# Where the work beside attention stands in the PE queue: between scores and values instead of after them

## The chip, the cores and the metric

The kernel runs on one core of a Trainium2 chip. The metric is device time in microseconds (us); the kernel before was timed three times, and 11980.78 us is the median (11979.94 to 11983.56). DMA moves data between HBM and the on-chip memories SBUF and PSUM. Engines are named as the profile does: PE (TensorE, matmuls), PEld (its weight loads), ACT (ScalarE), DVE (VectorE), POOL (GpSimd) and SP (SyncE, which here only issues DMAs). All data are float32.

## The reference, cut to what matters

Four images of 4096 tokens with 128 channels go through three layers: a state-space scan in three directions, an attention block with a small feed-forward part, and a mixture of 64 experts that pools tokens and scatters answers back. The change touches the attention block and what runs beside it:

```python
heads = u.reshape(4, 4096, 16, 8)                  # u: normalised tokens
q = qz_ring(heads + rx_theta)                      # cosines and running products
scores = einsum('bhsd,bhtd->bhst', q, q) / sqrt(8) # 16 heads, 4096 x 4096 each
attn = softmax(scores)
ctx = einsum('bhst,bhtd->bhsd', attn, q)
x1 = norm(u + ctx @ w_comb.T + b_comb)
zf = cos(x1[..., :8]) * cos(ry_theta)
x2 = norm(x1 + relu(zf @ w1.T + b1) @ w2.T + b2)   # then the layer's residual, norm, and gate logits
```

## The kernel before, in words

The program is written by one Python routine, `tile_kernel`, and the order in which instructions are recorded is the order in each engine's queue. It first makes the inputs of all scans and runs the scan of image 0, then the opening (angles, rings, queries) of image 0. Then come four attention loops, one for each image (`Attention.loop`). In the first three, the scan and opening of the next image and the closing work of the previous one are recorded beside the attention rounds. In the last (image 3) what runs beside it is the closing work of image 2 (`block.after(2)`), the choice and pooling of experts for images 0 to 2 (`Experts.search`, `choice`, `gather`), and the closing work of image 3 itself for those blocks of 512 queries that are done. After the loops come the last block's closing work and the experts' answers; I call it the tail.

One loop has 1024 rounds. A round treats four heads, 512 queries and 128 keys. `scores(i)` issues four matmuls (L955) into two PSUM tiles of two banks each, and for each tile one ACT exponential of 128x1024 (L960). `values(i)` issues four float32 matmuls (eight instructions in the trace, L969) which accumulate 32 rounds of one (head group, query block) pair in the one-bank tile acc. After the 32nd, `sums` copies acc to SBUF (L978, on ACT) and three rounds later stores it (L984, L987). The PSUM has three score tiles (six banks), one acc bank, and one bank for everything beside the rounds (`Bank`). The order within round i is: scores(i+1), values(i), sums, then `beside(i)`. So scores are one round ahead of values, and the exponential of round i+1 follows that of round i in ACT's queue.

Work beside is written as generators. Each `yield` is a step; a generator that is about to issue PE work yields the mark `PE`. `Bank.take` gives such a mark and waits until the bank is free. `flow` interleaves two such generators. `Pace.run(share)` adds a share to a credit and takes whole steps while there is credit: in the last loop 0.92 of a step in each round, whatever kind the step is.

A piece of PE work is all that one step issues. Pieces in the last loop, by name: co (L1072, two matmuls, 30 pieces), zt (L1093, four transposes, 15), h (L1107, one matmul of 8x512, 60), fo (L1118, four matmuls, 60), xT (L1140, four transposes, 14), lg (L1150, one matmul, 14), wt and pool (L1285 and L1296, four matmuls each, 24 of each). The scan's pieces in the first three loops are y (L582). Producers and consumers of these pieces are mostly on DVE: the norm (L836 to L842, with two POOL instructions at L48 and L49), products, and evictions from PSUM.

Of the kernel before, what the change touches and what calls it, by code (L numbers as in the profile page):

```python
# [16 lines left out]
P = 128  # L17
C = 128
L = 4096
NT = L // P  # L20
# [12 lines left out]
QB = 512  # L33
# [51 lines left out]
PE = "pe"  # L85
# [596 lines left out]
class Attention:  # L682
# [3 lines left out]
    def __init__(self, tc, ctx, w, gate, cols, ident, bank, dram, t1, w_out, sums, sz, x):  # L686
        nc = self.nc = tc.nc
        gate_w, gate_b = gate
        self.tc, self.cols, self.ident, self.bank, self.dram, self.t1 = tc, cols, ident, bank, dram, t1
        self.w_out, self.sums, self.sz, self.x = w_out, sums, sz, x  # L690
        const = ctx.enter_context(tc.tile_pool(name="a_const", bufs=1))
        self.half_pi = column(nc, const, math.pi / 2.0, "a_half_pi")

        def rows(name, n):
            t = const.tile([P, n], F32, name=f"bc_{name}")
            nc.scalar.dma_start(out=t, in_=w[name].partition_broadcast(P))
            return t

        self.theta = rows("rx_theta", D)
        self.bc = {k: rows(k, C) for k in ("b_comb", "b2", "g1", "beta1", "g2", "beta2")}  # L700
        self.b1 = const.tile([P, 4], F32, name="b1")
        nc.scalar.dma_start(out=self.b1, in_=w["b1"].rearrange("(f p) -> p f", p=P))
        self.cos_ry = const.tile([D, 3], F32, name="cos_ry")
        nc.scalar.dma_start(out=self.cos_ry[:, 0:1], in_=w["ry_theta"].unsqueeze(1))
        cosine(nc, self.cos_ry[:, 2:3], self.cos_ry[:, 0:1], self.cos_ry[:, 1:2], self.half_pi)
        self.w_comb = const.tile([P, C], F32, name="w_comb")
        self.w1 = const.tile([D, FFN], F32, name="w1")
        self.w2 = const.tile([P, 4, C], F32, name="w2")

        self.gate = const.tile([P, E], F32, name="gate")  # L710
        self.gate_b = const.tile([2 * E, 1], F32, name="gate_b")
        for k in range(2):
            nc.scalar.dma_start(out=self.gate_b[k * E : (k + 1) * E], in_=gate_b.unsqueeze(1))
        with tc.tile_pool(name="a_load", bufs=1) as load, tc.tile_pool(
            name="a_load_ps", bufs=2, space=PSUM
        ) as load_ps:
            raw = load.tile([P, C], F32, name="raw_comb")
            nc.sync.dma_start(out=raw, in_=w["w_comb"])
            ps = load_ps.tile([P, 512], F32, tag="ps", name="ps_comb")
            nc.tensor.transpose(ps[:, :C], raw, ident)  # L720
            nc.vector.tensor_copy(self.w_comb, ps[:, :C])
            raw = load.tile([P, 4, D], F32, name="raw_w1")
            nc.sync.dma_start(out=raw, in_=w["w1"].rearrange("(f p) d -> p f d", p=P))
            ps = load_ps.tile([P, 512], F32, tag="ps", name="ps_w1")
            for f in range(4):
                nc.tensor.transpose(ps[:D, f * P : (f + 1) * P], raw[:, f, :], ident)
            nc.vector.tensor_copy(self.w1, ps[:D])
            raw = load.tile([P, FFN], F32, name="raw_w2")
            nc.sync.dma_start(out=raw, in_=w["w2"])
            ps = load_ps.tile([P, 512], F32, tag="ps", name="ps_w2")  # L730
            for f in range(4):
                nc.tensor.transpose(ps[:, f * P : (f + 1) * P], raw[:, f * P : (f + 1) * P], ident)
            nc.vector.tensor_copy(self.w2.rearrange("p f c -> p (f c)"), ps)
            raw = load.tile([E, C], F32, name="raw_gate")
            nc.scalar.dma_start(out=raw, in_=gate_w)
            ps = load_ps.tile([P, 512], F32, tag="ps", name="ps_gate")
            nc.tensor.transpose(ps[:, :E], raw, ident[:E, :E])
            nc.vector.tensor_copy(self.gate, ps[:, :E])
        self.small = ctx.enter_context(tc.tile_pool(name="a_small", bufs=2))
        self.u, self.q, self.v, self.context, self.total, self.t2 = {}, {}, {}, {}, {}, {}  # L740
        self.xn, self.logits, self.angled, self.whole, self.closed = {}, {}, {}, {}, {}
        self.lag = 0
        self.round = column(nc, const, ROUND, "round"), column(nc, const, -ROUND, "minus_round")

    def begin(self, loop):
# [27 lines left out]
    def tokens(self, b, g, angles):  # L773


        nc = self.nc
# [6 lines left out]
        for m in range(2):  # L783
            rows = slice(m * P, (m + 1) * P)
# [35 lines left out]
        turned(nc, a, turns.rearrange("p h d -> p (h d)"), self.round if self.n == 4 else None)  # L820
        self.angled[b] += 1
        yield

    def settle(self, n=1):

# [80 lines left out]
    def loop(self, b, beside, by_block=False):  # L906


        nc = self.nc
        self.context[b] = self.dram.tile([P, L], F32, name=f"d_ctx_{b}")  # L910
        self.total[b] = self.dram.tile([L // QB, H, QB], F32, name=f"d_sum_{b}")
        self.whole[b] = 0
# [62 lines left out]
        def sums(j, qb, i):  # L975

            av = self.mid.tile([P, QB], F32, tag="av", name=f"av_{b}_{j}_{qb}")
            nc.scalar.copy(av, accs.pop((j, qb)))  # L978
            cut = slice(qb * QB, (qb + 1) * QB)

            def store():
                for k in range(4):
                    h = 4 * k + j
                    nc.gpsimd.dma_start(  # L984
                        out=self.context[b][h * D : h * D + D, cut], in_=av[32 * k : 32 * k + D, :]
                    )
                nc.gpsimd.dma_start(  # L987
                    out=self.total[b][qb].rearrange("(k j) t -> j k t", j=4)[j], in_=av[D::32, :]
                )
                if by_block and j == 3:  # L990
                    self.whole[b] = qb + 1

            later[i + 3] = store
# [5 lines left out]
        for i, (j, qb, kc) in enumerate(rounds):  # L999
            if i % 4 == 0:  # L1000
                fetch(i // 4 + 3)
            if i + 1 < len(rounds):
                scores(i + 1)
            values(i)
            if kc == NT - 1:
                sums(j, qb, i)
            if kc == NT - 12 and i + 12 < len(rounds):
                masked(*rounds[i + 12][:2])
            if i in later:
                later.pop(i)()  # L1010
            beside(i)
        for i in sorted(later):
            later[i]()
        self.whole[b] = L // QB

    def after(self, b, gs=range(L // QB), to=None):
# [68 lines left out]
        def second(g):  # L1085
# [4 lines left out]
            nc.sync.dma_start(out=t, in_=tiles[:, cut, :])  # L1090
            ps = yield from self.bank.take(f"zt_{b}_{g}")
            for k in range(4):
                nc.tensor.transpose(ps[:D, k * P : (k + 1) * P], z[:, g * 4 + k, :], self.ident)  # L1093
            yield
            zT = self.piece([D, 512], "p0", name=f"zT_{b}_{g}")
# [8 lines left out]
            h = self.one.tile([P, 4, 512], F32, tag="h", bufs=max(1, self.n - 1), name=f"h_{b}_{g}")  # L1104
            for f in range(4):
                ps = yield from self.bank.take(f"h_{b}_{g}_{f}")
                nc.tensor.matmul(ps, self.w1[:, f * P : (f + 1) * P], zT, start=True, stop=True)  # L1107
                yield
                if self.n == 2:
                    nc.vector.tensor_scalar(h[:, f, :], ps, self.b1[:, f : f + 1], 0.0, ALU.add, ALU.max)  # L1110
                else:
                    nc.scalar.activation(h[:, f, :], ps, AF.Relu, bias=self.b1[:, f : f + 1])
                self.bank.leave()
            yield from self.settle()
            for k in range(4):
                ps = yield from self.bank.take(f"fo_{b}_{g}_{k}")
                for f in range(4):
                    nc.tensor.matmul(  # L1118
                        ps[:, :C], h[:, f, k * P : (k + 1) * P], self.w2[:, f, :], start=(f == 0), stop=(f == 3)
                    )  # L1120
                yield
                nc.vector.tensor_add(u[:, k, :], u[:, k, :], ps[:, :C])
                self.bank.leave()
# [13 lines left out]
            yield from self.settle()  # L1137
            ps = yield from self.bank.take(f"xT_{b}_{g}")
            for k in range(4):
                nc.tensor.transpose(ps[:, k * P : (k + 1) * P], u[:, k, :], self.ident)  # L1140
            yield
            xT = self.piece([P, 512], "p0", name=f"xT_{b}_{g}")
# [4 lines left out]
            yield from self.settle()  # L1147
            ps = yield from self.bank.take(f"lg_{b}_{g}")
            rows = slice(E, 2 * E) if to else slice(0, E)
            nc.tensor.matmul(ps[rows], self.gate, xT, start=True, stop=True)  # L1150
            yield
            if to:
                for t in to:
# [283 lines left out]
class Pace:  # L1437


    def __init__(self, *parts):  # L1440
        self.parts, self.credit, self.done, self.then = chain(*parts), 0.0, False, None

    def run(self, share):
        self.credit += share
        while self.credit >= 1 and not self.done:
            self.credit -= 1
            self.then = next(self.parts, self)
            self.done = self.then is self

    def rest(self):  # L1450
        while not self.done:
# [3 lines left out]
def tile_kernel(tc, ctx, x, in_proj_w, dirs, out_proj_w, attn, gate, weight1, weight2, out):  # L1455


    nc = tc.nc
# [81 lines left out]
    with tc.manual_schedule():  # L1540
# [6 lines left out]
            block.after(nb - 1, range(0, 4)), block.after(nb - 1, range(4, 6)), block.after(nb - 1, range(6, blocks - 1)),  # L1547
            experts.search(pairs[-1], blocks - 1),
        )
        block.loop(nb - 1, lambda i: last.run(0.92), True)  # L1550
        last.rest()
    loop.close()
    with ExitStack() as end:
        block.bank = Bank(end.enter_context(tc.tile_pool(name="end_ps", bufs=7, space=PSUM)), 7)
# [47 lines left out]
```

## Time and profile before

The profile is of one execution, whose own time was 11985.97 us; its span from first to last instruction is 11984.3 us. Times inside the profile count from the span's start.

| stretch (us from start) | length | PE busy | DVE busy | ACT busy | granted PE clock |
|---|---|---|---|---|---|
| first loop, 2437 to 4831 | 2394 | 2223 | 2058 | 2326 | 0.98 |
| second loop, 4876 to 7248 | 2372 | 2245 | 2065 | 2299 | 0.98 |
| third loop, 7292 to 9620 | 2328 | 2219 | 1889 | 2260 | 0.98 |
| last loop, 9622 to 11734 | 2112 | 2071 | 361 | 1940 | 1.00 |
| tail, 11734 to 11984 | 250 | 128 | 86 | 32 | 0.67 |

"Busy" is the time in which at least one instruction of the engine is recorded as running. Matmuls overlap and their ends are modelled, so a busy PE may still have room. In the timeline, a line gives the start, how long the merged run of instructions lasted, the engine, the code line, operation, output<-input, and in brackets how long the engine was idle before it and what ended that. In lists of waits, a line says which engine's which line waited for which, the total, the count and the longest.

### The profile page before, as it was taken

The numbers are of one execution on the slowest core, as the hardware profiler recorded it, in microseconds if no ns is written. First come the engines' busy times: TensorE is split into PE (matmuls) and PEld (weight loads), VectorE is DVE, ScalarE is ACT, GpSimd is POOL, SyncE is SP. The second block draws the span as 40 slices with busy tenths as digits, with TensorE's granted clock in tenths as the row PEclk, the third lists the DMA queues.
The fourth block names the chain that finished last, engine by engine and source line by source line (L and its number), as shares of the span: only waits on it lengthen the run. The fifth ranks groups of instructions, "written<-read, shape, count | busy, mean of one in ns | idle before, by whom it ended". The sixth has DMA issues, their size and how long they took to land.

```text
span 11984.3 us, 184513 instructions
## 1 busy us (share of the span) xinstructions
PE 10801.0 (90%) x69190; PEld 3648.6 (30%) x69190; DVE 8666.3 (72%) x8841; ACT 10457.4 (87%) x10884; POOL 3068.7 (26%) x4017
## 2 busy tenths in 40 slices
PE   7898888489999999899999998999999999999995
PEld 3333333222222222233333222233332223333323
DVE  6999999889888877898889878989898321101123
ACT  5776777389999999899999988999999999999992
POOL 2323243222232322323334223233232110100011
PEclk9898989699999999999999999999999999999997
DMA  5666666655656565665565655655555332222125
GB/s 159 206 185 181 188 177 187 199 159 151 157 150 158 136 163 162 166 158 151 145 152 141 158 169 165 156 147 148 144 144 134 123 109 67 74 69 78 61 71 182
DMA packets 835831, 1747.64 MB, mean 146 GB/s; under 512 B 141070, under 2 KB 373574, under 8 KB 834678
## 3 DMA queue, kind: packets, MB, share of 16 engines
q1 hardware_dynamic: 649438, 1318.65, 41.5%
q0 software_dynamic: 144000, 307.48, 8.2%
q10 hardware_dynamic: 41496, 109.71, 3.5%
q8 instruction: 543, 8.90, 0.3%
q14 instruction: 354, 2.90, 0.1%
HBM read 1379.76 MB, written 355.47 MB: 145 GB/s over the span
## 4 chain that ended last, share of the span: by engine, by line
PE 62%; ACT 12%; issue 9%; DVE 8%; DMA 7%; SPq 1%; POOL 0%; ACTq 0%; DVEq 0%; POOLq 0%
PE acc L969 31%; PE s L955 15%; ACT e L960 7%; PE y L582 5%; DVE h L550 3%; PE cv L390 3%; PE sp L448 3%; DMA delta<-d_delta 2%; PE fo L1118 1%; PE xd L404 1%; PE h L1107 1%; DMA y<-d_y 1%; DVE dB L541 1%; ACT dA L534 1%; ACT delta L534 1%
## 5 line engine op out<-in xcount | busy, mean ns | idle before, releaser
L960 ACT ACTIVATE e<-s 128x1024 f32<-128x1024 f32 x8192 | 7778.6, 1102 | 366.5 <-PE s L955 322.0
L969 PE MATMUL acc<-e,val 128*32 128x512 f32 x32768 | 5681.9, 614 | 79.7 <-ACT av L978 79.0
L955 PE MATMUL s<-qm,key 32*128 32x512 f32 x16384 | 2783.4, 501 | 373.2 <-ACT e L960 311.5
L955 PEld LDWEIGHTS s<-qm,key 32*128 32x128 f32 x16384 | 1067.2, 183 | 3628.7 <-issue 1953.2
L552 POOL COPY ends<-h 128x1 f32<-128x1 f32 x1152 | 1299.0, 1130 | 2685.2 <-DVE h L550 2682.1
L969 PEld LDWEIGHTS acc<-e,val 128*32 128x32 f32 x32768 | 1027.7, 109 | 2007.6 <-issue 1015.7
L550 DVE TENSOR_TENSOR_SCAN h<-delta,ends,du 128x1024 f32<-128x1024 f32 x576 | 1349.6, 2343 | 113.8 <-ACT delta L534 95.9
L550 DVE TENSOR_TENSOR_SCAN h<-dA,ends,dB 128x1024 f32<-128x1024 f32 x576 | 1349.6, 2343 | 46.5 <-ACT dA L534 43.4
L541 DVE TENSOR_TENSOR dB<-du,B 128x1024 f32<-128x1024 f32 x768 | 927.8, 1208 | 603.2 <-PE y L582 387.4
L534 ACT ACTIVATE dA<-delta,A 128x1024 f32<-128x1024 f32 x768 | 938.0, 1221 | 176.9 <-DMA delta<-d_delta 169.8
L534 ACT ACTIVATE delta<-delta,A 128x1024 f32<-128x1024 f32 x768 | 939.0, 1223 | 132.7 <-PE y L582 124.6
L541 DVE TENSOR_TENSOR du<-du,B 128x1024 f32<-128x1024 f32 x768 | 920.4, 1198 | 30.4 <-DMA B<-d_bc 30.4
L555 DVE TENSOR_TENSOR du<-h,C 128x1024 f32<-128x1024 f32 x768 | 934.6, 1217 | 0.1
L555 DVE TENSOR_TENSOR dB<-h,C 128x1024 f32<-128x1024 f32 x768 | 934.2, 1216 | 0.0
L582 PE MATMUL y<-dB,sel 128*32 128x256 f32 x6144 | 724.3, 394 | 33.4 <-DVE ring L879 20.8
L582 PE MATMUL y<-du,sel 128*32 128x256 f32 x6144 | 718.1, 390 | 12.6 <-DVE du L555 12.5
L390 PE MATMUL cv<-xn,conv 128*128 128x512 f32 x1024 | 487.9, 629 | 32.5 <-DVE xn L325 17.3
L984 POOL DMA_DIRECT2D d_ctx<-av x512 | 260.1, 520 | 926.9 <-ACT av L978 920.2
L611 POOL DMA_DIRECT2D d_y<-o x512 | 329.5, 674 | 521.0 <-DVE o L598 470.7
L550 DVE TENSOR_TENSOR_SCAN h<-delta,du 128x1024 f32<-128x1024 f32 x192 | 438.2, 2282 | 19.6 <-ACT delta L534 11.0
L550 DVE TENSOR_TENSOR_SCAN h<-dA,dB 128x1024 f32<-128x1024 f32 x192 | 438.2, 2282 | 16.7 <-ACT dA L534 15.1
L576 POOL DMA_DIRECT2D d_du<-x_delta x272 | 154.7, 569 | 1104.4 <-DVE x_delta L575 1033.8
(260 smaller groups left out, 7862.8 us busy)
## 6 DMA issues: line engine op xcount, KB each, us to landing
delta<-d_delta SPq DMA_DIRECT2D x768, 512.0 KB
du<-d_du SPq DMA_DIRECT2D x576, 512.0 KB
du<-d_du ACTq DMA_DIRECT2D x192, 512.0 KB
key<-d_q SPq DMA_DIRECT2D x352, 256.0 KB
d_u<-u POOLq DMA_DIRECT2D x48, 1024.0 KB, 5.6
B<-d_bc SPq DMA_DIRECT2D x96, 512.0 KB
C<-d_bc SPq DMA_DIRECT2D x96, 512.0 KB
d_delta<-r POOLq DMA_DIRECT2D x48, 1024.0 KB, 5.5
```

The source lines that it names most:

```text
L390: nc.tensor.matmul(ps[:, cut], w["conv"][:, k, m * P : (m + 1) * P], reads(k, g), start=(k == 0), stop=(k == 3))
L448: nc.tensor.matmul(ps[:, cut], sign, t[:, m, cut], start=(i == 0), stop=(i == 2))
L534: nc.scalar.activation(tiles["delta", s], t, AF.Exp, scale=A)
L541: nc.vector.tensor_mul(tiles["du", s], du, spread[order, c, "B", j % 2])
L550: nc.vector.tensor_tensor_scan(h, dA, dB, first, ALU.mult, ALU.add)
L552: nc.gpsimd.tensor_copy(ends[order, c][:, at : at + 1], h[:, T - 1 :])
L555: nc.vector.tensor_mul(dB, h, spread[order, c, "C", j % 2])
L582: nc.tensor.matmul(y[32 * g : 32 * g + 32, : T // 4], self.sel[:, j // 2, :], hC[:, 256 * g : 256 * g + 256], start=(j == 0), stop=(j == 3),)
L611: nc.gpsimd.dma_start(out=to.rearrange("p (i j) -> p i j", i=SLICES)[:, :, at : at + n], in_=rows.rearrange("p (i j) -> p i j", i=SLICES),)
L955: nc.tensor.matmul(s_ps[:, k, :], keys[f"{i // 4}"][rows, cut].bitcast(F32R), queries[j, qb][rows, :].bitcast(F32R), start=True, stop=True,)
L960: nc.scalar.activation(e, s_ps, AF.Exp, scale=1.0 / math.sqrt(D))
L969: nc.tensor.matmul(accs[j, qb][32 * k : 32 * k + 32, :], v[:, k * VW : k * VW + 32], es[i][k // 2][:, k % 2, :], start=(kc == 0), stop=(kc ...
```

## The change

It has four parts.

1. In every loop the order in a round becomes scores(i+1), the query load, the late store, `beside(i)`, and only then values(i) and sums.
2. In the last loop alone (`by_block`), `sums` copies acc with DVE instead of ACT.
3. PE pieces are cut in halves. For h and lg each matmul becomes two of 256 columns (in all loops, as instructions); for zt, fo, xT, h and lg a `pause` lies between the halves. `pause` yields only while `cut` is set, which is in the last loop; wt, pool and co are not cut.
4. In the last loop the pace is `turn(1.5, i % 3 > 0 or i > 830)`: 1.5 steps of credit in a round, at most 3 saved up; at most one PE piece in a round, and none in each third round up to round 830.

```diff
+    def pause(self):
+        if self.cut:
+            yield PE
...
     def loop(self, b, beside, by_block=False):
         nc = self.nc
+        self.cut = by_block
...
-            nc.scalar.copy(av, accs.pop((j, qb)))
+            (nc.vector.tensor_copy if by_block else nc.scalar.copy)(av, accs.pop((j, qb)))
...
             if i + 1 < len(rounds):
                 scores(i + 1)
-            values(i)
-            if kc == NT - 1:
-                sums(j, qb, i)
             if kc == NT - 12 and i + 12 < len(rounds):
                 masked(*rounds[i + 12][:2])
             if i in later:
                 later.pop(i)()
             beside(i)
+            values(i)
+            if kc == NT - 1:
+                sums(j, qb, i)
...
             for k in range(4):
+                if k == 2:
+                    yield from self.pause()
                 nc.tensor.transpose(ps[:D, k * P : (k + 1) * P], z[:, g * 4 + k, :], self.ident)
...
-                nc.tensor.matmul(ps, self.w1[:, f * P : (f + 1) * P], zT, start=True, stop=True)
+                for part in range(2):
+                    cols = slice(part * QB // 2, (part + 1) * QB // 2)
+                    if part:
+                        yield from self.pause()
+                    nc.tensor.matmul(ps[:, cols], self.w1[:, f * P : (f + 1) * P], zT[:, cols], start=True, stop=True)
...
                 for f in range(4):
+                    if f == 2:
+                        yield from self.pause()
                     nc.tensor.matmul(
                         ps[:, :C], h[:, f, k * P : (k + 1) * P], self.w2[:, f, :], start=(f == 0), stop=(f == 3)
                     )
...
+    def step(self):
+        self.credit -= 1
+        self.then = next(self.parts, self)
+        self.done = self.then is self
...
+    def turn(self, share, free):
+        self.credit = min(self.credit + share, 3.0)
+        while self.credit >= 1 and not self.done and (free or self.then is not PE):
+            free = free and self.then is not PE
+            self.step()
...
-        block.loop(nb - 1, lambda i: last.run(0.92), True)
+        block.loop(nb - 1, lambda i: last.turn(1.5, i % 3 > 0 or i > 830), True)
         last.rest()
+        block.cut = False
```

xT is cut as zt is, and lg as h is.

More of the change, by code (lines that the diff above doesn't have):

```diff
@@ L741, in __init__ @@
         self.xn, self.logits, self.angled, self.whole, self.closed = {}, {}, {}, {}, {}
-        self.lag = 0
+        self.lag, self.cut = 0, False
         self.round = column(nc, const, ROUND, "round"), column(nc, const, -ROUND, "minus_round")
@@ L1139, in second @@
             for k in range(4):
+                if k == 2:
+                    yield from self.pause()
                 nc.tensor.transpose(ps[:, k * P : (k + 1) * P], u[:, k, :], self.ident)
@@ L1149, in second @@
             rows = slice(E, 2 * E) if to else slice(0, E)
-            nc.tensor.matmul(ps[rows], self.gate, xT, start=True, stop=True)
+            for part in range(2):
+                cols = slice(part * QB // 2, (part + 1) * QB // 2)
+                if part:
+                    yield from self.pause()
+                nc.tensor.matmul(ps[rows, cols], self.gate, xT[:, cols], start=True, stop=True)
             yield
@@ L1445, in run @@
         while self.credit >= 1 and not self.done:
-            self.credit -= 1
-            self.then = next(self.parts, self)
-            self.done = self.then is self
+            self.step()
[3 more added lines that the diff above has]
+            free = free and self.then is not PE
+            self.step()
     def rest(self):
```

## The prediction

> **What bounds the kernel now.** I read the page first (shares, slices, groups), then busy time and waits by stretch, then single rounds in the timeline.
>
> ```profile
> PE 10801.0 (90%) x69190; PEld 3648.6 (30%) x69190; DVE 8666.3 (72%) x8841; ACT 10457.4 (87%) x10884; POOL 3068.7 (26%) x4017
> ...
> ACT  5776777389999999899999988999999999999992
> ...
> L960 ACT ACTIVATE e<-s 128x1024 f32<-128x1024 f32 x8192 | 7778.6, 1102 | 366.5 <-PE s L955 322.0
> L955 PE MATMUL s<-qm,key 32*128 32x512 f32 x16384 | 2783.4, 501 | 373.2 <-ACT e L960 311.5
> ```
>
> PE looks like the bound (90%), but in the loops ACT is as full, and each of the two waits some 320 us for the other. By stretch, ACT's idle time ahead of exponentials is 65, 68 and 60 us in the first three loops (one wait of 20 to 26 us each stands at the loop's start), and in the last loop, 9622 to 11734:
>
> ```profile
> ACT e L960 <- PE s L955: 132.2, 187, 1.0
> ACT e L960 <- PE h L1107: 39.4, 60, 0.9
> ```
>
> That is 172 us in 247 short gaps, none over 1.0. A gap, in the last loop:
>
> ```profile
> 10446.91 0.51 PE L955 MATMUL s<-qm,key 32*128 32x512 f32 x4
> 10447.35 1.46 PE L969 MATMUL acc<-e,val 128*32 128x512 f32 x8
> 10447.76 0.14 PEld L969 LDWEIGHTS acc<-e,val 128*32 128x32 f32 x4 [0.27 <-ACT e L960]
> 10448.74 1.16 PE L1118 MATMUL fo<-w,h 128*128 128x128 f32 x8
> 10449.83 0.51 PE L955 MATMUL s<-qm,key 32*128 32x512 f32 x4
> ...
> 10450.27 1.07 PE L969 MATMUL acc<-e,val 128*32 128x512 f32 x8
> 10450.43 5.60 ACT L960 ACTIVATE e<-s 128x1024 f32<-128x1024 f32 x6 [0.89 <-PE s L955]
> 10451.27 0.73 PE L955 MATMUL s<-qm,key 32*128 32x512 f32 x4
> ```
>
> A plain round takes PE 1.83 us (10446.91 to 10448.74): scores 0.44, half of the values, a wait for the second exponential, the other half. When nothing is waited for it takes 1.44 (10449.83 to 10451.27): scores 0.43, values 0.99 to 1.00. ACT needs 1.82 for its two exponentials (a run of 14 lasts 12.94, its members start 0.91 apart). So plain rounds are bound by ACT and PE has 0.4 us to spare, but inside the values, where nothing uses it. The fo piece stands after the values, pushes the next scores back by 1.09, and ACT runs dry for 0.89. I sorted the trace's gaps in this loop by the piece before them: fo 60 gaps of 0.89 (53.3 us), h 60 of 0.66 (39.4), pool and wt 48 of 0.84 (40.1), co 30 of 0.42 (12.7), lg 14 of 0.80 (11.2), xT 13 of 0.39 (5.1), zt 15 of 0.32 (4.8), after a copy of acc 11 of 0.49 (5.4): 172 in all.
>
> [...] the last loop's PE is 98% busy (2071 of 2112 us), yet a round can shrink from 1.83 to 1.44. [...] So a piece that waits now also holds the values behind it; the trace agrees in so far as no L969 overtakes a piece. [...] the like-shaped eviction here (L1143) takes 692 ns, and I use that.
>
> **Last loop, part by part.** Take the gap above. With the new order scores start at 10446.91, the piece at 10447.34. A whole piece of 1.03 (wt, pool) ends at 10448.37; by then both exponentials of the values are there, so values take 0.99, scores follow at 10449.36, and ACT, which starts 0.60 after scores (10450.43 less 10449.83), at 10449.96. It ran dry at 10449.54 (10450.43 less 0.89): gap 0.42 instead of 0.84. A half of fo (0.545) gives 10449.48: no gap.
> - Halves (fo, h, lg, xT, zt) and co (0.6 us, two matmuls): 126.5 us of gaps go. A round with a half costs PE 1.44 + 0.55 = 1.99, over ACT's 1.82, so two in succession use up the slack; the free third round pays it back (2 x 1.99 + 1.44 = 5.42, below 3 x 1.82 = 5.46). Past round 830 there is no free round: some 75 pieces x 0.15 = at most 11; I take 8. Saved 118.
> - wt and pool stay whole: 48 x 0.42 = 20 saved.
> - Copy of acc to DVE: on ACT it is 0.62 long and delays the next exponential by 0.47 (starts 11600.69 and 11601.16): 32 x 0.47 = 15 saved. The DVE copy, 0.69, is hidden because DVE is busy 17% there (361 of 2112); without that cover values wait for acc, as they do now (0.82 each, 24.8 in sum). The 5.4 us after copies I leave.
> - The extra h and lg matmuls: two more weight loads of 0.18 and 0.13, overlapped; nothing. In the first three loops too.
> - The faster pace has a price. In the built programs the pieces stand closer to their producers: xT of the last group of each batch follows its fo by 4, 4, 4 and 5 rounds, before by 8, 8, 7 and after the loop. In the old trace the producer chain (evictions, two norms with POOL in each) left 3.2, 3.2 and 0.9 us of slack in 16.5, 16.5 and 14.5, so it needs 13.3 to 13.6, about 12.7 from a half. Four rounds are 7.4: waits of 5.3, 5.3, 5.3, 3.6 = 20. wt follows the choice in 10 and 9 rounds instead of 15, with 2.2 and 2.5 of slack then; MAX8 (4.4), exponentials (about 6), match and select (9.7) make about 20.4 against 15: 2 x 5 = 10. The first co of the loop moves from round 9, where it was just on time, to 6: 5. All are in front of values, so ACT pays: 35 lost. Other pieces keep over 1 us by the same count.
>
> Sum: 118 + 20 + 15 - 35 = 118 saved.
>
> **Tail.** Before, the closing work of the last early block ended after the loop, so its MAX8 stood in DVE's queue ahead of the last block's norm.
>
> ```profile
> 11754.28 0.69 DVE L1064 TENSOR_TENSOR cT<-cT,part 128x512 f32<-128x512 f32 x1 [4.57 <-DMA part<-d_share]
> ...
> 11760.32 3.89 DVE L1235 MAX8 best<-prob 64x8 f32<-64x3584 f32 x1 [0.25 <-DMA prob<-d_lg]
> 11764.23 1.12 DVE L842 TENSOR_SCALAR x<-x,mv_x,rs_x 128x128 f32<-128x128 f32 x4
> ```
>
> In the changed program that work ends at round 955. The norm then waits only for POOL (1.43), 2.8 earlier, and the reciprocal that feeds cT is no longer behind an xT copy, some 3 earlier. Saved 6.
>
> **First three loops.** The record of steps beside is the same there; only its place against values changes. Of their ACT gaps I count, apart from the starts, 82 that follow a piece (y, out, qT, h, co); each can shrink by the same 0.42 or to nothing: 33 saved (10 if most of them come from late data, 55 if the following rounds gain as well). The y pieces now stand 1.4 us earlier against DVE; the smallest distance from a product on DVE to its y matmul in these loops is 18.9 us, so none waits. The ACT copy comes after the round's ACT work beside (1.25 us); values of the next round then wait longer for acc, but PE issued the next scores before, so ACT has two exponentials meanwhile: nothing, at worst 3 x 32 x 0.3 = 29. DMA loads on SP and stores on POOL keep their order; the query load and the late store pass only values.
>
> **Sum.** 118 + 6 + 33 = 157 off the profiled execution's 11985.97: 11829. The median of the runs shown is 5.2 below that execution: 11824, 1.3% faster.
>
> **Rivals.**
> - PE is the bound, order is indifferent (0.05): for it speaks the busy share of 98%; against it rounds of 1.44. Left are the copy and the tail: 11980.8 - 21 = 11960, which is within 0.2%.
> - The pace overruns its producers (0.12): waits three times as long as I count, 105 instead of 35, because the DVE chain gets longer when copies of acc and two groups share the queue. Gain 87: 11894.
> - Slower (0.03): late data in front of values. A piece whose data come after the point where values would have ended delays values by their 0.99. Place: the 568 y pieces of the first three loops, where DVE is 81 to 87% busy. From 157 / 0.99 = 159 waiting pieces on the gain is gone; with half of them waiting, 284 x 0.99 = 281 - 157 = 124 slower: 12105. Against it: 18.9 us of slack.
>
> **How the numbers follow.** Main case 0.80. Its range: waits in the last loop 15 to 80, first loops 55 to -10 (gain), the saving past round 830 +-5: 11775 to 11885. Taking in the second rival's centre, 11770 to 11895. A difference under 0.2% (24 us) can't be told from none here. Faster: 0.80 + 0.12 = 0.92; same 0.05; slower 0.03.
>
> **What would show it.** Right: in the last loop gaps after fo, h, lg near zero, after wt and pool 0.4, sum 60 to 80 us; plain rounds still 1.82; L978 on DVE; waits of PE on L842 and L1273 of some 5 us at six places; the last loop near 1994 long; the first three 5 to 20 shorter each. Wrong: gaps of ACT that grow with single waits over 5 us at more places; exponentials further apart than 0.91; waits of y on DVE.

## The result, and the profile after

The changed kernel takes 11896.83 us (median of four runs, 11894.23 to 11900.66), the kernel before 11982.17 us beside it (four runs, 11979.94 to 11989.24): a ratio of 0.9928 [0.9912, 0.9944], 0.7% or some 85 us faster. The forecast was 11824, with a range of 11770 to 11895; the time lies 1.8 us above the range. The profiled execution took 11898.45 us, its span is 11896.7.

The lines of the page that answer to those shown of before (busy time, ACT by slices, exponentials, scores; the columns are busy time and mean ns of one, then the idle time ahead of them):

```profile
PE 10382.9 (87%) x69510; PEld 3480.6 (29%) x69510; DVE 8691.8 (73%) x8873; ACT 10442.6 (88%) x10852; POOL 3213.1 (27%) x4017
...
ACT  5776777489999999899999998999999999999992
...
L966 ACT ACTIVATE e<-s 128x1024 f32<-128x1024 f32 x8192 | 7782.5, 1108 | 304.1 <-PE s L961 293.2
...
L961 PE MATMUL s<-qm,key 32*128 32x512 f32 x16384 | 2652.5, 500 | 622.2 <-ACT e L966 564.3
```

PE's waits for an exponential rose from 311.5 to 564.3 us: the new order does free PE. ACT's waits for scores fell from 322.0 to 293.2, and all its idle time ahead of exponentials from 366.5 to 304.1. From the start of the first exponential of each loop to the start of the last, in the two traces:

| stretch, us | before | after | difference | forecast |
|---|---|---|---|---|
| first three loops | 2393.7 + 2371.3 + 2327.1 | 2389.7 + 2376.4 + 2322.6 | -3.4 | -33 |
| last loop | 2111.7 | 2031.2 | -80.5 | -118 |
| after the last exponential | 250.6 | 250.4 | -0.2 | -6 |

Each of the three terms is smaller than forecast. In the last loop (9615 to 11647 in this trace), the waits of ACT, as line, releaser, sum, count and longest:

```profile
ACT e L966 <- PE s L961: 96.6, 84, 8.2
```

Before these were 247 gaps, none over 1.0 us; now they are 84, the longest 8.2. What PE waits for there:

```profile
PE xT L1156 <- DVE x1r L847: 15.1, 4, 4.2
PE acc L975 <- DVE av L984: 12.5, 15, 3.2
PE wt L1305 <- DVE chosen L1293: 7.9, 2, 4.6
PE co L1078 <- DVE cT L1070: 6.4, 1, 6.4
PE h L1119 <- DVE h L1122: 5.0, 3, 3.2
PE co L1078 <- DVE x L1081: 3.0, 3, 2.1
```

In the last loop of before PE waited for no producer of a piece. The late xT (four), wt (two) and first co stand where the forecast put them.

For the finer count I sorted, in each trace, the last loop's distances between starts of successive exponentials by the piece issued between them, and summed what exceeds 0.904 us (the distance when ACT is never dry). Distances with other work of ACT between the two exponentials, such as a copy of acc, are left out, and so are differences of a few ns. A sum can move by some 2 us with the piece that a gap is booked to. These sums are time of the loop; per gap they are about 0.17 more than the idle time that the forecast counted (fo: 1.06 against 0.89). It gives, before and after: fo 63.4 and 25.1, h 50.1 and 16.3, pool and wt 49.2 and 41.0, co 18.3 and 19.0, lg 13.7 and 4.7, xT 7.4 and 21.6, zt 7.2 and 2.5, no piece 7.1 and 15.8; in all 216.8 and 146.3. The distances with other work of ACT in them exceed 0.904 by 37.3 us in all before and 22.3 after: the copies of acc that left ACT are 15 us.

### The profile page after: what moved, and what is told of

It reads as the page before. It is cut to its first block, busy times and chain, and to the rows that moved or that the text cites. A ratio compares the mean times of both kernels' runs of the same rounds, so it can differ in the third digit from the quotient of the medians.

```text
span 11896.7 us, 185104 instructions
## 1 busy us (share of the span) xinstructions
PE 10382.9 (87%) x69510; PEld 3480.6 (29%) x69510; DVE 8691.8 (73%) x8873; ACT 10442.6 (88%) x10852; POOL 3213.1 (27%) x4017
## 4 chain that ended last, share of the span: by engine, by line
PE 41%; ACT 26%; issue 14%; DVE 11%; DMA 7%; POOL 1%; SPq 1%; ACTq 0%; DVEq 0%; POOLq 0%
PE acc L975 20%; ACT e L966 19%; PE s L961 9%; DVE h L550 4%; PE cv L390 3%; PE sp L448 3%; DMA delta<-d_delta 2%; PE y L582 1%; ACT dA L534 1%; DMA du<-d_du 1%; PE xd L404 1%; ACT delta L534 1%; DVE dB L541 1%; PE fo L1132 1%; DMA y<-d_y 1%
## 5 line engine op out<-in xcount | busy, mean ns | idle before, releaser
L966 ACT ACTIVATE e<-s 128x1024 f32<-128x1024 f32 x8192 | 7782.5, 1108 | 304.1 <-PE s L961 293.2
L975 PE MATMUL acc<-e,val 128*32 128x512 f32 x32768 | 5253.9, 615 | 98.8 <-ACT av L984 85.9
L961 PE MATMUL s<-qm,key 32*128 32x512 f32 x16384 | 2652.5, 500 | 622.2 <-ACT e L966 564.3
L961 PEld LDWEIGHTS s<-qm,key 32*128 32x128 f32 x16384 | 1015.8, 184 | 4474.4 <-issue 2511.4
L552 POOL COPY ends<-h 128x1 f32<-128x1 f32 x1152 | 1440.0, 1252 | 2622.5 <-DVE h L550 2619.7
L975 PEld LDWEIGHTS acc<-e,val 128*32 128x32 f32 x32768 | 973.8, 109 | 1606.5 <-issue 789.6
L534 ACT ACTIVATE dA<-delta,A 128x1024 f32<-128x1024 f32 x768 | 938.4, 1222 | 168.6 <-DMA delta<-d_delta 160.0
L534 ACT ACTIVATE delta<-delta,A 128x1024 f32<-128x1024 f32 x768 | 939.9, 1224 | 135.2 <-PE y L582 126.8
L582 PE MATMUL y<-dB,sel 128*32 128x256 f32 x6144 | 508.7, 404 | 37.1 <-DVE ring L884 20.8
L582 PE MATMUL y<-du,sel 128*32 128x256 f32 x6144 | 490.1, 392 | 12.6 <-DVE du L555 12.6
```

The source lines that it names most:

```text
L534: nc.scalar.activation(tiles["delta", s], t, AF.Exp, scale=A)
L552: nc.gpsimd.tensor_copy(ends[order, c][:, at : at + 1], h[:, T - 1 :])
L582: nc.tensor.matmul(y[32 * g : 32 * g + 32, : T // 4], self.sel[:, j // 2, :], hC[:, 256 * g : 256 * g + 256], start=(j == 0), stop=(j == 3),)
L961: nc.tensor.matmul(s_ps[:, k, :], keys[f"{i // 4}"][rows, cut].bitcast(F32R), queries[j, qb][rows, :].bitcast(F32R), start=True, stop=True,)
L966: nc.scalar.activation(e, s_ps, AF.Exp, scale=1.0 / math.sqrt(D))
L975: nc.tensor.matmul(accs[j, qb][32 * k : 32 * k + 32, :], v[:, k * VW : k * VW + 32], es[i][k // 2][:, k % 2, :], start=(kc == 0), stop=(kc ...
```

## The experiments

Edits are against the changed kernel unless they say "against before". "Last loop" is from its first to its last exponential; before 2111.7, after 2031.2.

### The order alone, in all loops and in the last one

Against before, e1_order_all moves `values(i)` and `sums` behind `beside(i)` and changes nothing else; e2_order_last does it only where `by_block` is set.

```diff
-            values(i)
-            if kc == NT - 1:
-                sums(j, qb, i)
...
             beside(i)
+            values(i)
+            if kc == NT - 1:
+                sums(j, qb, i)
```

> The kernel before with the new order in every loop and nothing else of the change: old pace of 0.92, no halves, copy of acc on ACT. Theory (a piece between scores and values costs 0.42 us less of ACT's time, no more; in the first three loops ACT's own work beside already covers the pieces; the new pace costs most of what the halves bring): the first three loops together within 10 us of before, the last loop 90 to 105 us shorter, whole ratio 0.991 to 0.993, that is as fast as the full change. Rival A (the halves carry the gain): last loop only 30 to 50 shorter, ratio 0.996 to 0.998. Rival B (the first three loops lose by late data what they gain): they differ from before by more than 15 us.

> As the run before, but the new order in the last loop only. Theory: same time as with the order in all loops, within 10 us, since the first three loops are indifferent to it. Rival (my prediction's step): 33 us slower than with the order in all loops. Rival B (late data cost the first loops something): faster than with the order in all loops.

Measured: e1 11883.57, 0.9910 [0.9896, 0.9923]; e2 11888.88, 0.9916 [0.9902, 0.9929]. The last loop is 2010.7 in both, 101.0 shorter than before and 20.5 shorter than with the whole change. The first three loops sum to 7095.7 and 7088.9, against 7092.1 before: in sum the order is worth nothing there. In e1's last loop ACT's waits are all short:

```profile
ACT e L960 <- PE s L955: 69.2, 167, 1.6
```

By piece, the mean excess after fo fell from 1.06 to 0.62, after pool from 1.05 to 0.60, after wt from 1.01 to 0.59, after h from 0.85 to 0.38: 0.42 to 0.47 each, and the forecast had read 0.42 off one round for a whole piece (0.84 to 0.42). So the mechanism of the order is as told, and the order is the part of the change that pays.

### The change with the old order

g3_after_old_order keeps halves, pace and DVE copy, and puts values and sums back where they were.

```diff
+            values(i)
+            if kc == NT - 1:
+                sums(j, qb, i)
...
             beside(i)
-            values(i)
-            if kc == NT - 1:
-                sums(j, qb, i)
```

> The changed kernel with values ahead of the work beside again, all else as changed (halves, pace, DVE copy). Theory (the order alone carries the gain): a half behind values costs ACT 0.44 us, two of them as much as a whole one, and the pace costs 20 to 50: last loop 2115 to 2150, at or above the kernel before. Rival (halves and pace carry part of the gain themselves): last loop under 2100.

Measured: 11986.27, 0.9995 [0.9987, 1.0004]; last loop 2114.2. Without the order the rest brings nothing that can be told from none: halves still leave some 0.4 after fo and 0.3 after h, and there are twice as many; the late xT and wt are there too.

### The pieces whole

e3_after_whole makes the pause empty, so that the order, the pace of one piece in two of three rounds, and the DVE copy remain.

```diff
     def pause(self):
-        if self.cut:
-            yield PE
+        yield from ()
```

> The changed kernel with its pieces whole again in time (no pause between the halves; the h and lg matmuls stay two of 256 columns each). Pace, order and DVE copy as changed. Theory (halves of fo still cost 0.2 us each and h a little, whole pieces 0.4 to 0.5): the last loop 20 to 35 us longer than with halves, so 0.995 to 0.996 of before. Rival (halves are free and whole pieces cost 0.42): 50 to 60 us longer. If the halves bring nothing: same.

Measured: 11963.76, 0.9978 [0.9968, 0.9988]; last loop 2087.6, 56.4 longer than with halves. That is the number of the rival in the expectation (50 to 60), but not its reason: fo, h and lg, which were halved, account for some 30 us, within the theory's 20 to 35, and co, which is whole in both kernels, for over 20. As I read it, without pauses the same pace runs through the closing work faster and catches up with the attention that feeds it. PE's waits in the last loop:

```profile
PE co L1077 <- DVE cT L1069: 22.6, 4, 6.7
PE acc L974 <- DVE av L983: 17.7, 18, 7.0
PE xT L1155 <- DVE x1r L846: 10.8, 3, 4.2
PE wt L1304 <- DVE chosen L1292: 8.9, 2, 4.6
```

All four batches now start with a co that waits for its sums. So this run doesn't isolate the halves; it shows that pace and piece size belong together.

### Time for the producers

e4_after_spare adds empty steps in the last loop ahead of the pieces that were late, so that other pieces go first: 7 ahead of the first co of a batch and of the last xT, 8 after each choice.

```diff
+    def spare(self, n):
+        for _ in range(n if self.cut else 0):
+            yield
...
+            yield from self.spare(7 if g == gs[0] else 0)
             for half in range(2):
                 ps = yield from self.bank.take(f"co_{b}_{g}_{half}")
...
+            yield from self.spare(7 if g == gs[-1] else 0)
             ps = yield from self.bank.take(f"xT_{b}_{g}")
...
+        yield from self.block.spare(8)
```

> The changed kernel with 7 or 8 empty steps ahead of the first co and the last xT of each batch and after the choice, in the last loop only: the same work, later. Theory (late producers in front of values cost 40 to 60 us, more than the waits themselves because the granted clock of PE falls to a half for some 6 us after a wait): the last loop 35 to 55 us shorter than with the change, about 0.988 to 0.990 of before, PE's waits on the norm's and the choice's output gone. Rival (the waits only move, because the work is done late at the end): same as the change within 10.

Measured: 11865.85, 0.9896 [0.9882, 0.9909]; last loop 1990.7, 40.5 shorter than after and 20.0 shorter than the order alone. The waits for x1r and chosen are gone from PE's list:

```profile
PE acc L979 <- DVE av L988: 10.0, 15, 5.0
PE co L1083 <- DVE x L1086: 6.5, 4, 3.2
PE h L1124 <- DVE h L1127: 4.4, 3, 3.2
PE co L1083 <- DVE cT L1074: 2.7, 1, 2.7
```

By piece, xT falls from 21.6 to 0.6, wt from 26.5 to 13.9, h from 16.3 to 11.7; fo stays (25.1 and 24.4). The late data cost 40.5 us, and the forecast had 35.

### The copy of acc

f1_order_dve is e1 with the copy on DVE, as the change has it; g1_after_act is the changed kernel with the copy back on ACT:

```diff
-            (nc.vector.tensor_copy if by_block else nc.scalar.copy)(av, accs.pop((j, qb)))
+            nc.scalar.copy(av, accs.pop((j, qb)))
```

> The kernel with only the new order in all loops, and in the last loop the copy of acc on DVE besides. Prediction's term: 15 us shorter than with the order alone (32 copies x 0.47 on ACT), nothing given back. Rival (read from the changed kernel's gaps, where the sum after copies rose from 5 to 10 us, partly since a DVE queue busy with norms makes values wait for acc): only 5 to 10 us shorter. Last loop 1996 or 2001 to 2006.

> The changed kernel with one part undone: acc is copied by ACT again in the last loop. Prediction's term: 15 us slower than the change. Rival (values wait for acc behind DVE's queue[...]): the gain and the loss cancel, the same as the change within 8 us; ACT's copies cost 15 again and the waits of values on the DVE copy (12.5 us) and part of the late gaps go. Last loop 2025 to 2046.

Measured: f1 11879.98, 0.9911 [0.9896, 0.9926], last loop 2005.0, only 5.7 shorter than e1. g1 11898.2, 0.9924 [0.9911, 0.9936], which can't be told from after; its last loop is 2022.2, 9.0 shorter than after. In g1 the 31 copies on ACT cost their 15 us again, but h falls from 16.3 to 2.6 and "no piece" from 15.8 to 5.3; PE waits there for the copy 27 times, never over 0.9 us, and 0.2 us in all for an eviction of h. In after the three longest waits for the copy (2.25, 3.20 and 2.35 us) end with a DVE copy of 0.69 that stood behind other work of DVE (a norm twice, the scaling after one once); its two longest waits for h (1.65 and 3.19) end with an eviction behind a norm's L847, which each time had itself waited 3.19 us for POOL. Why the waits for h go with the DVE copy was not shown. The clock stands at 0.50 for 68.3 us of g1's last loop and for 99.0 of after's. In the last loop the copy on DVE thus gains 6 us at the slow pace and costs 9 at the fast one; the whole times of g1 and after don't show the 9, as g1's trace is 3.8 longer in the first three loops and 3.4 ahead of them.

### A piece in each second round, and the weights later

f3_second_count is e4 with a free round after each piece: `i % 2 == 0` in place of `i % 3 > 0 or i > 830`, and a piece counted when it is issued and not by the mark ahead of it. f2_spare_late is e4 with the experts' first weights asked for after the tail's sine, f4_second_count_late is f3 with that.

```diff
         while self.credit >= 1 and not self.done and (free or self.then is not PE):
-            free = free and self.then is not PE
+            n = bank.count
             self.step()
+            free = free and bank.count == n
...
-        block.loop(nb - 1, lambda i: last.turn(1.5, i % 3 > 0 or i > 830), True)
+        block.loop(nb - 1, lambda i: last.turn(1.5, i % 2 == 0, block.bank), True)
...
                 for i, _ in enumerate(closing):
-                    if i == 2:
+                    if i == 13:
                         experts.prefetch(room, nc.scalar)
```

> The changed kernel with spare steps, with a piece in each second round only (the whole loop), where a step that only finds the bank taken does not use up the turn. Theory (a half costs PE 2.07 us in its round and the next plain round gives back 0.3, so two in three rounds are more than ACT's 1.82 and one in two is not): the gaps after halves of fo, h and lg go from 41 us to under 12, last loop 1960 to 1970, ratio 0.9865 to 0.988. Rival (a half costs 0.2 wherever it stands): last loop as with spare steps, 1985 to 1995.

> The changed kernel with spare steps, and the 12 to 15 weight loads that ACT issues after the loop recorded behind the tail's sine instead of ahead of it. Theory (the tail didn't shrink since these loads now start 2 us after the loop and the small loads of sum, share and context wait behind them in the DMA engines): the first co comes 6 to 8 us earlier after the last exponential, tail 243 to 246 instead of 250. Rival (the small loads are slow for another reason): tail unchanged. Rival 2 (the late weights hold up the experts): tail longer.

> The run before and the late weight loads together. If both theories hold, 5 to 7 us shorter than the run before, all of it in the tail. If the loads were no cause: the same.

Measured: f3 11871.49, 0.9901 [0.9886, 0.9916], last loop 1989.8; f2 11859.53, 0.9894 [0.9877, 0.9910]; f4 11859.42, 0.9895 [0.9880, 0.9910]. The loop of f3 is no shorter than that of e4. fo fell to 16.0 and h to 4.3, in the direction that the free round should give; with 3.5 for lg that is 24 us, where under 12 was expected. And "no piece" rose to 31.8: four stalls of ACT of 6 to 8 us on the DVE copy. One of them, in the timeline of f3:

```profile
10680.35 2.40 PE L981 MATMUL acc<-e,val 128*32 128x512 f32 x8
...
10682.01 4.40 DVE L1291 MATCH_REPLACE8 chosen<-top,prob 64x4096 f32<-64x4096 f32 x1
...
10686.87 4.41 DVE L1301 SCALAR_TENSOR_TENSOR chosen<-chosen,prob 64x4096 f32<-64x4096 f32 x1
10691.21 0.68 DVE L990 COPY av<-acc 128x512 f32<-128x512 f32 x1
10691.94 1.94 PE L981 MATMUL acc<-e,val 128*32 128x512 f32 x8 [6.59 <-DVE av L990]
...
10694.70 1.94 ACT L972 ACTIVATE e<-s 128x1024 f32<-128x1024 f32 x2 [7.32 <-PE s L967]
```

The copy is ready to go when the values end, stands behind the choice's match and select in DVE's queue, and the one acc bank holds up PE for 6.59 us and ACT for 7.32.

The tail of f2 shows two things. In after and in e4 the experts' weights (L1333, L1336) leave ACT's queue 2.3 us after the last exponential (19.1 in e1, where closing work of an early block still runs then, and, as I read it, holds their room in SBUF); the tail's small transfers then share the DMA engines with them. From the end of the last values to the start of co (11648.5 to 11674.0) the DMA engines are 81% busy, where they are 28% busy in the first 21 us of the tail of before (11734 to 11755). The tail of after:

```profile
11648.50 0.40 ACTq L1333 DMA_DIRECT2D w<-in_L_ffn_weight_dram  x1
...
11656.88 0.33 SPq L1050 DMA_DIRECT2D sum<-d_sum  x1
...
11662.43 0.55 DVE L1053 RECIPROCAL sum<-sum 128x64 f32<-128x64 f32 x1 [13.23 <-DMA w<-in_L_ffn_weight_dram]
...
11674.20 2.05 PE L1078 MATMUL co<-w_comb,cT 128*128 128x128 f32 x8 [25.75 <-DVE cT L1070]
...
11684.90 1.02 PE L1101 MATMUL zt<-ident,z 128*8 128x128 f32 x4 [8.64 <-ACT z L1189]
```

And the tail of f2, with the weights after the sine:

```profile
11621.39 0.55 DVE L1057 RECIPROCAL sum<-sum 128x64 f32<-128x64 f32 x1 [6.09 <-DMA sum<-d_sum]
...
11629.76 2.04 PE L1083 MATMUL co<-w_comb,cT 128*128 128x128 f32 x8 [15.20 <-DVE cT L1074]
...
11641.13 7.59 ACTq L1343 DMA_DIRECT2D w<-in_L_ffn_weight_dram  x4
...
11657.70 2.42 ACT L1129 ACTIVATE h<-h,b 128x512 f32<-128x512 f32 x4 [17.31 <-DMA w<-in_L_ffn_weight_dram]
11658.44 5.87 PEld L1137 LDWEIGHTS fo<-w,h 128*128 128x128 f32 x32 [9.68 <-ACT h L1129]
```

The wait for cT falls from 25.75 to 15.20, but the weights' issues now stand in ACT's queue ahead of the relu of h, and fo waits 9 us for that. The tail is 248.3, against 249.7 in e4: won and lost again. f4 is 12 us faster than f3, but not by its tail (250.8 and 251.3 in the traces): most of it stands in the first three loops (7086.7 and 7095.5), which the edit doesn't touch, so it says nothing of the weights.

### The pieces put together

g2_best is f3 with the copy on ACT and the weights asked for after the relus (`i == 28`).

> What the runs so far point to: new order, halves, a piece in each second round with turns counted only when a piece is issued, spare steps at the late producers, acc copied by ACT, and the weight loads of the tail recorded on ACT behind its last four relus. Theory: against the same with the DVE copy, ACT pays 15 us for copies and saves the 28 us of waits on the DVE copy and some 10 us of low clock behind them, last loop 1960 to 1975; the tail loses 6 to 10 us of its 250, since the small loads come early and ACT's relus no longer stand behind 15 DMA issues. Ratio 0.986 to 0.988, the fastest of all. Rival (the DVE waits only uncover other gaps): last loop 1985 to 2000.

Measured: 11831.55, 0.9869 [0.9856, 0.9883]; last loop 1972.7, tail 241.2. It beats both kernels, and is some 65 us below after. Its loop is 17.1 shorter than that of f3, and the copy on ACT is the only edit between the two that touches the loop. PE's waits in its last loop (9620 to 11587) hold no DVE copy any more, and ACT's are

```profile
ACT e L972 <- PE s L967: 36.4, 60, 4.5
```

and the idle time ahead of its exponentials is 38 us in all, where after has 105 and before 172. The tail gains 9.2 against after, as co starts 16.9 us after the start of the last exponential (28.0 in after) and the fo of its last block follows the relus at once (11624.67, the last relu starting at 11624.78).

## Why the forecast missed, point by point

The direction and the main mechanism were right (e1 shows the order's gain per piece, 0.42 to 0.47 for 0.42; g3 shows that it is needed). The sum was 157, and the gain is 84 by the medians and 87 by the two traces. The terms:

**First three loops, 33 forecast, 3.4 measured: this step failed.** I counted 82 gaps of ACT after a piece, gave each the 0.42 of the last loop, and let none grow. e1, which has the order there, and e2, which hasn't, have the same loops within 7 us. Busy time by stretch (length, then PE, PEld, DVE, ACT), first of before, then of after:

```profile
2437.00:4831.00 2394.00, 2223.45 (x15725) 692.72 (x15726) 2057.92 (x1729) 2325.76 (x2495) 661.87 (x897) 0.98 0.59 153
4876.00:7248.00 2372.00, 2244.61 (x15939) 719.56 (x15934) 2065.05 (x2095) 2298.87 (x2467) 747.40 (x938) 0.98 0.59 153
```

```profile
2437.00:4826.00 2389.00, 2131.25 (x15722) 634.14 (x15722) 2057.36 (x1730) 2324.83 (x2494) 716.24 (x897) 0.98 0.59 153
4870.00:7246.00 2376.00, 2139.07 (x16012) 673.90 (x16010) 2066.77 (x2096) 2297.76 (x2466) 768.24 (x938) 0.97 0.59 153
```

PE sheds 92 and 106 us, and the loop stays as long: PE's waits for exponentials take up what it saves. In the first loop, before and after:

```profile
PE s L955 <- ACT e L960: 129.2, 198, 5.8
PE s L961 <- ACT e L966: 203.2, 370, 6.6
```

ACT is 97% busy in both, and the idle time ahead of its exponentials in the three loops, without their starts, is as before (128.7 and 131.0 us), but it has moved. A piece stands between two exponentials at 844 places. At 786 of them ACT has other work there too, an exponential of the scan (L534, 1.25 us) in all but two, which covers most of these pieces. At the 58 others the idle time fell from 47.9 to 28.8 us: there the order gains. At the 786 it rose from 53.7 to 75.1. All traces agree: those with the old order in these loops (before, e2, g3) have 46 to 53 and 47 to 54 us at the two kinds of places, the ten with the new one 26 to 38 and 62 to 76. PE's waits in these loops rose too: for work of DVE from 52.6 us in 22 waits to 75.6 in 41, and for ACT's copies of acc from 54.2 to 85.9. With the new order a piece that waits holds up the values behind it: in the last loop of after, an xT that waited 4.23 us started at 10481.78, and the values behind it only at 10482.44, 5 us after the scores ahead of both (10477.05). So the main case failed in letting the gain stand at every gap and pricing late data at nothing in these loops; late data were its third rival, and its low case of 10. That these waits make up ACT's loss is my reading; no run isolates them.

**Last loop, halves and co, 118 forecast.** With the producers in time (e4), spacing above 0.904 fell by 39.0 at fo, 38.4 at h, 8.6 at lg, 6.8 at xT, 6.9 at zt and by nothing at co: 99.7 in all. Even this owes something to luck, as two errors go against each other. The forecast priced these gaps at their idle time, 126.5 us, where the loop lost 160.1 by them (spacing above 0.904), so there was 33.6 more to gain. And it held that all but 8 would go, where 60.4 stay. The second error has two parts. "A round with a half costs 1.99, and the third round pays it back": a round of after, in the timeline:

```profile
9998.31 18.24 ACT L966 ACTIVATE e<-s 128x1024 f32<-128x1024 f32 x19
...
10000.63 0.50 PE L961 MATMUL s<-qm,key 32*128 32x512 f32 x4
...
10001.07 0.71 PE L1132 MATMUL fo<-w,h 128*128 128x128 f32 x4
...
10002.70 0.50 PE L961 MATMUL s<-qm,key 32*128 32x512 f32 x4
...
10004.20 0.67 PE L961 MATMUL s<-qm,key 32*128 32x512 f32 x4
...
10006.44 0.51 PE L961 MATMUL s<-qm,key 32*128 32x512 f32 x4
```

The half pushes the values back by 0.64 (10001.07 to 10001.71), not 0.545, so the first round takes 2.07; the plain one takes 1.50; the third, again with a half, 2.24, as its scores take 0.60 (10004.20 to 10004.80) where the first's take 0.44. Three rounds are 5.81 us, not 5.42, against 5.46 for ACT. PE is the bound by 0.35 in three rounds, and it shows in no idle gap: the 19 exponentials are one run of 18.24 us, 0.96 each. It costs 0.21 per half, 25 us at 119 of them. The forecast's sign for this, "exponentials further apart than 0.91", was the right thing to look for. With a free round after each half (g2) it falls to 0.14, 16.4 us. And co: its median excess fell from 0.64 to 0.21, but a few long waits bring the sum back (18.3 before, 19.1 in e4, 8.5 in e1). In e4 PE waits four times, 6.5 us in all, for DVE to empty the bank (L1086), now that the next round may take it, and once, 2.7 us, for cT.

**wt and pool, 20 forecast:** right. 49.2 before, 28.5 in e4, where their data are in time.

**DVE copy, 15 forecast:** 5.7 with the order alone (f1), and in the changed kernel a loss of 9.0 in the last loop (g1). ACT did save the 15, and waits on DVE gave them back. The step "hidden because DVE is busy 17%" took a mean share for a wait: a copy that values need comes up behind whatever DVE is doing, and the largest of these took 4.40 and 4.41 us (f3).

**Late data, -35 forecast:** 40.5 (e4 against after). The places were right; the four waits of ACT at xT are 5.5, 5.5, 5.5 and 2.9 (5.3 three times and 3.6 forecast). Each is longer than PE's own wait (at most 4.2). What I had not counted are waits at h, the first of them 1.65 us, and a lower clock behind a wait. The granted clock (third last column) around the first wait of h, from 9828.98 in after:

```profile
9828.00:9831.00 3.00, 2.02 (x15) 0.80 (x16) 0.93 (x3) 1.46 (x2) 0.60 (x1) 0.99 0.25 93
9831.00:9834.00 3.00, 3.00 (x18) 0.69 (x13) 0.75 (x1) 1.94 (x2) 0.00 (x0) 0.50 0.00 0
9834.00:9837.00 3.00, 3.00 (x16) 0.56 (x16) 0.00 (x0) 1.94 (x2) 0.00 (x0) 0.50 0.00 0
9837.00:9840.00 3.00, 3.00 (x26) 0.81 (x22) 0.00 (x0) 2.73 (x3) 0.00 (x0) 0.87 0.00 0
```

```profile
9828.98 0.69 PE L1119 MATMUL h<-zT,w 8*128 8x256 f32 x2 [1.65 <-DVE h L1122]
...
9831.92 1.94 PE L975 MATMUL acc<-e,val 128*32 128x512 f32 x8
...
9834.68 1.94 ACT L966 ACTIVATE e<-s 128x1024 f32<-128x1024 f32 x2 [1.50 <-PE s L961]
...
9837.27 5.61 ACT L966 ACTIVATE e<-s 128x1024 f32<-128x1024 f32 x6 [0.65 <-PE s L961]
```

After PE has waited 1.65 us, the clock is at 0.50 for two of these stretches of 3 us, and values take 1.94 instead of 1.07. ACT runs dry twice more, by 1.50 and 0.65. The dip that follows this wait lasts 6.83 us, and the others of this loop 3.41, 6.83 or 10.24. The length of the wait alone doesn't settle whether one follows: after waits of 1.84 and 2.35 us in the same loop (ended at 10511.18 and 11272.23) the clock stayed at 1.00.

**Tail, 6 forecast, 0.2 measured.** The saving itself came: from co to zt it took 17.2 us before and takes 10.7 now, with MAX8 no longer ahead of the norm. But co starts 28.0 us after the start of the last exponential, where it was 21.6: the experts' weights, which now start 2.3 us after it, slow the small transfers ahead of co. I had no term for these transfers. f2 and g2 show that the delay comes with the weights (co at 17.4 in f2 and 16.9 in g2).

Together: 30 from the first loops, 18 from halves and co (118 - 99.7), 6 from the tail and 5.5 from late data are 59.5 of gain forecast and not had; 157 - 59.5 = 97.5, against the 84.1 that the three stretches of the table give. The 13.4 between them fall to the copy, which by this sum brought 1.6 of its 15 us; alone it brought 5.7 in f1 and lost 9.0 in g1, so terms interact and the split is rough. How much of the 40.5 is the clock stays open. It stands at 0.50 for 20.5 us of the last loop in before and in e1, for 99.0 in after and 58.0 in e4; my estimate from these figures is at most some 20 of the 40.5 us, half of the 41.0 between after and e4.

The range didn't follow from its own parts. Added up, they give 157 + 20 + 22 + 5 = 204 at the fast end, 11777, which the range has as 11775, and 157 - 45 - 43 - 5 = 64 at the slow end, 11917, where it stopped at 11885 (11895 with the rival).

The rival "the pace overruns its producers" gave 11894 and came nearest in size, but not for its reason: the waits were near what the main case held, and the loss lay elsewhere. "PE is the bound, order is indifferent" is refuted by e1 for the last loop; the length of the first three loops is indifferent to the order, but by a gain and a loss that cancel.

## What to carry to other kernels

A gain per gap that was read in one stage holds only where the same engine is dry for the same reason: before multiplying, sort each stage's gaps by what else stands in the round, and ask which engine is full and which gaps can grow. Work that is put in front of the main stream must find its data ready, so give the producers spare rounds when the pace rises, and keep an eviction that the main stream needs off an engine with operations of several microseconds (4.40 and 4.41 here, behind which one copy held PE up for 6.59). When something ends earlier, look for the transfers that its end releases.

## What the runs showed of the hardware

- A wait of PE of 1.65 us among dense matmuls (after, ended at 9828.98) was followed by a granted clock of 0.50 for 6.83 us; beside waits of 2.10, 3.19, 4.23 and 4.63 us in the same trace (9703, 10310, 10482, 10526) it was 0.50 too, for 3.41, 6.83, 6.83 and 10.24 us. After waits of 1.84 and 2.35 us (10511, 11272) it was not.
- Half of an fo piece (two matmuls of 128x128, four instructions) costs PE 0.64 us ahead of values (after), where the whole piece costs 1.09 in the trace of before and, ahead of values too, in e1: half of this group leaves 59% of its time.
- With the weights in flight, the reciprocal of the sums started 16.2 us after the start of the last exponential (16.0 in e4), and without them 9.0 (after and f2; 9.2 in f4).
